# Last chunk of a graph layer: attention terms from unscaled rows, the 20-row tile ranked as columns, its X W made one pass later

## Chip, cores and metric

The kernel runs on one core of one Trainium2 chip. The metric is the device time of one launch in microseconds; the median of the runs shown is 1096.91 us.

## The reference

There are N = 2708 nodes with 128 features, a sparse non-negative matrix A (2708 x 2708), and four layers, each `x = layernorm(x + layer(x, A))`. The change lies where layer 0 ends and layer 1 begins.

```
layer 0:  y = d2 * x                      (d2 from the degrees and from 4 near neighbours S)
          out = d2 * ((S + A) @ y) @ W2 + b2
          x = layernorm(x + out)
layer 1:  XW = x @ W
          c = XW @ a[:128],  r = XW @ a[128:]            one number per node each
          den[i,j] = exp(leaky_relu(r[i] + c[j], 0.01))
          num = A @ den;   att = den / num
          H = A @ (att @ XW);   x = layernorm(x + H)
layers 2, 3: one product with A each
```

`den` has 2708 x 2708 entries, but r[i] + c[j] >= 0 or < 0 decides between two products of one-node terms. The kernel therefore sorts the nodes by c: it needs the rank of every c[j] among all of them, ties broken by the node's number.

## The kernel before

**Tiles, chunks, passes.** The nodes are cut into T = 22 tiles of 128 rows (the last, tile 21, has 20 rows) and C = 6 chunks of columns: four of 512, one of 384 (tiles 16 to 18), and the last of 276 (tiles 19, 20, 21). A transposed copy of A is streamed from memory panel by panel through a ring of four slots; six of its row tiles stay resident. A product of the whole of A with something 128 wide is a pass (`by_panels`, its matmul is L204). Pass 1 makes degrees and A x; then the neighbour stage finds four near nodes for every node (MAX8 and FIND_INDEX8 on VectorE, matmul L642 on TensorE); pass 2 makes (S + A) y; the third pass (`part_sum`, L1176) makes sums of A over runs of nodes in the order of c; then blocks of att are made and multiplied (block layer, L1423 and L1280), and three more passes follow.

**Order.** In pass 2 and after, the order on TensorE, VectorE and ScalarE is the order of the program (`manual_schedule`). In pass 2 the list `due` holds work by tick: one tick for each matmul of the pass, and `at(n, f, ...)` says at which tick `f` is issued. `end_pass2` files the work of a finished chunk; what is left when the matmuls end is issued by `due.flush()`, so that the whole tail of the last chunk comes then. GpSimd (POOL) and SyncE have their own queues, in order too. On each engine an instruction that waits holds back all behind it.

**What a chunk goes through.** `finish` adds the neighbour sums (`add_near`, L692) and copies the result to hT (L832). `norm0` multiplies by W2, adds to xs and normalizes: statistics on VectorE, the inverse root for the last chunk by POOL's pow (L253), then xs is scaled (L277). `turn` transposes xs (L737) and ScalarE copies it to xT (L739). `find_c` multiplies by a matrix whose columns all are W a (w_c, L744), so that c stands in every partition; ScalarE copies it to c_row (tile hT, L745), and VectorE picks the diagonals into cc (L749), one value per row. `times_w` makes X W and r (L757), `keep_xw` stores X W to memory through POOL (L763).

**Ranks.** `compare(t)` writes a mask: for each row of tile t, which columns up to its own tile have a c at least as large (L779; for tile 21 in the form that also sums, L774), and counts ties inside the tile (L781). `rank_rows` sums a mask along its rows on ScalarE (L792), `rank_columns` sums it along its columns on TensorE into rk (L797). After the flush, rk_f = after - rows_d - rk + rows_m is the rank (L918 to L923).

**From the ranks to the third pass.** `pick_c` finds the c at chosen ranks (L932 to L937), `to_all` spreads them over the partitions by a matmul (L943), `on_all` builds the row gb by 22 transposes of gb_col (L908) and six ScalarE copies (L915), and VectorE makes lc (L972 to L977), the weights of the third pass. `between(c, i0)` puts further work between its matmuls: at (0, 8) `find_blocks`, at (1, 4) the placing matmuls js (L1023), at (2, 4) `ranked`, which lets POOL clear xws and fetch X W rows in sorted order (L1047, L890). The matmul of lone_part (L1243) stands behind the first chunk's part sums.

**Buffers.** Masks have three buffers; small results go through `mis_tile`, three PSUM buffers in turn. `near` (128 x 22 x 8) is used by the neighbour stage only.

Of the kernel before, what the change touches and what calls it, by code (L numbers as in the profile page):

```python
# [8 lines left out]
F32 = mybir.dt.float32  # L9
U32 = mybir.dt.uint32  # L10
I32 = mybir.dt.int32
BF16 = mybir.dt.bfloat16
# [4 lines left out]
P = 128  # L17
# [13 lines left out]
class Due:  # L31
# [5 lines left out]
    def at(self, n, f, *args):  # L37
        self.work.append((n, len(self.work), f, args))
        self.work.sort(key=lambda w: w[:2])
# [13 lines left out]
def kernel(  # L53
# [213 lines left out]
    def normalize(ts, xs, power=False):  # L267

        t0, t1 = ts[0], ts[-1] + 1
        for t in ts:  # L270
            st = small.tile([P, 6], F32, tag="st", name="st")
            nc.vector.bn_stats(st[: pw[t]], xs[: pw[t], t, :])
            nc.vector.bn_aggr(mv[: pw[t], t, :], st[: pw[t]])
        rstd = small.tile([P, 4], F32, tag="rstd", name="rstd")
        inv_sqrt_of(rstd[:, : t1 - t0], mv[:, t0:t1, 1], LN_EPS, power)
        for t in ts:
            nc.vector.tensor_scalar(  # L277
                xs[: pw[t], t, :], xs[: pw[t], t, :], mv[: pw[t], t, 0:1], rstd[: pw[t], t - t0 : t - t0 + 1],
                op0=ALU.subtract, op1=ALU.mult,
            )  # L280
# [28 lines left out]
    def atile(shape, name, dt=F32):  # L309
        return att1.tile([P] + shape, dt, tag=name, name=name)  # L310
# [53 lines left out]
    with tc.tile_pool(name="knn", bufs=1) as knn:  # L364
# [185 lines left out]
            )  # L550
        w_c = atile([P], "w_c")
        nc.vector.tensor_copy(w_c, wae[:, D + 1 :].to_broadcast([P, P]))

        y2 = big.tile([P, T, D], F32, tag="y", name="y2")

# [147 lines left out]


    if LAST:
        nc.gpsimd.memset(xwe[:, FULL, :], 0.0)
        nc.gpsimd.memset(cc[:, FULL:], 0.0)


    c_row = hT  # L710
    rows_m = atile([T], "rows_m")
    rows_d = atile([T], "rows_d")
    nc.vector.memset(rows_d, 0.0)
    add_bias(b2_sb)
    rk = rk_pool.tile([P, T], F32, tag="rk", name="rk")

    def norm0(ts, power=False):
        po = mis_tile()
        for k, t in enumerate(ts):
            nc.tensor.matmul(  # L720
                po[: pw[t], k * D : (k + 1) * D], lhsT=hT[:, t * P : t * P + pw[t]], rhs=w2_sb, start=True, stop=True
            )
        for k, t in enumerate(ts):
            p = pw[t]
            nc.vector.scalar_tensor_tensor(
                xs[:p, t, :], po[:p, k * D : (k + 1) * D], d2inv[:p, t : t + 1], xs[:p, t, :],
                op0=ALU.mult, op1=ALU.add,
            )
        normalize(ts, xs, power)

    xTs, masks = {}, {}

    def turn(c):
        pt = mis_tile()
        for t in chunk_tiles[c]:
            o = t * P - starts[c]
            nc.tensor.transpose(pt[:, o : o + pw[t]], xs[: pw[t], t, :], ident[: pw[t], : pw[t]])  # L737
        xTs[c] = sum_pool.tile([P, CW], F32, tag="xT", name="xT", bufs=3)
        nc.scalar.copy(xTs[c][:, : cw[c]], pt[:, : cw[c]])  # L739

    def find_c(c):

# [17 lines left out]
    def keep_xw(c):  # L760
# [5 lines left out]
        if t1 <= ts[-1]:  # L766
            nc.gpsimd.dma_start(xw_rows[FULL * P :, :], xwe[:LAST, FULL, :D])

    def compare(t):
        p, o = pw[t], t * P  # L770
        s = cc[:p, t : t + 1]
        mask = masks[t] = sum_pool.tile([P, N], BF16, tag="mask", name="mask", bufs=3)
        if t in by_dve:
            nc.vector.tensor_scalar(  # L774
                mask[:p, : o + p], c_row[:p, : o + p], s, 0.0, op0=ALU.is_ge, op1=ALU.add,
                accum_out=rows_m[:p, t : t + 1],
            )
        else:
            nc.vector.tensor_scalar(mask[:p, : o + p], c_row[:p, : o + p], s, None, op0=ALU.is_ge)  # L779
        eq = small.tile([P, P], F32, tag="junk", name="eq")  # L780
        nc.vector.scalar_tensor_tensor(  # L781
            eq[:p, :p], c_row[:p, o : o + p], s, not_before[:p, :p], op0=ALU.is_equal, op1=ALU.mult,
            accum_out=rows_d[:p, t : t + 1],
        )

    by_dve = (T - 1,)

    def rank_rows(t):
        p, w = pw[t], t * P + pw[t]
        if t not in by_dve:  # L790
            junk = sum_pool.tile([P, N], BF16, tag="copy", name="junk")
            nc.scalar.activation(junk[:p, :w], masks[t][:p, :w], AF.Copy, accum_out=rows_m[:p, t : t + 1])  # L792

    def rank_columns(t):
        p = pw[t]
        for u in range(t):
            nc.tensor.matmul(  # L797
                rk[:, u : u + 1], lhsT=masks[t][:p, u * P : (u + 1) * P], rhs=ones_b[:p, :1],
                start=(t == 1 and u == 0), stop=(t == T - 1), skip_group_check=True,
            )  # L800


    def exp_table():
        tc.keep_in_program_order(nc.scalar.preload_act_table_set("natural_log_exp_and_others"))
# [1 line left out]
    gb_col = atile([T], "gb_col")  # L806

    def find_r():
        nc.vector.tensor_copy(rr, xwe[:, :, D])

    def exp_r():
        nc.scalar.activation(e_r, rr, AF.Exp)
# [12 lines left out]
    def end_pass2(c, acc):  # L825
        n = max(due.n + 1, near_at[chunk_tiles[c][-1]] + 3, ended[-1] + 16)
        ended.append(n)
        ts = chunk_tiles[c]

        def finish():  # L830
            add_near(c, acc)
            nc.scalar.copy(hT[:, cols[c]], acc[:, : cw[c]])  # L832

        at(n, finish)
        if c < C - 1:
            at(n + 2, norm0, ts)
            at(n + 9, turn, c)
            at(n + 11, find_c, c)
            for k, t in enumerate(ts):
                at(n + 13 + 2 * k, compare, t)  # L840
                at(n + 14 + 2 * k, times_w, c, t)
                if k == len(ts) - 1:
                    at(n + 14 + 2 * k, keep_xw, c)
                if c == C - 2 and k == len(ts) - 1:
                    behind_last.append(t)
                else:
                    at(n + 16 + 2 * k, rank_rows, t)
                if t:
                    at(n + 17 + 2 * k, rank_columns, t)
        else:  # L850
            for t in behind_last:
                at(n + 1, rank_rows, t)
            at(n + 1, exp_table)
            at(n + 2, norm0, ts, True)
            at(n + 3, turn, c)
            at(n + 4, find_c, c)
            for t in ts:
                at(n + 4, times_w, c, t)
            at(n + 4, keep_xw, c)
            for k, t in enumerate(ts):  # L860
                if k == len(ts) - 1:
                    at(n + 5 + k, find_r)
                at(n + 5 + k, compare, t)
                at(n + 5 + k, rank_rows, t)
                at(n + 6 + k, rank_columns, t)
            at(n + 6 + len(ts), exp_r)

    with tc.manual_schedule(engines={nc.tensor.engine, nc.vector.engine, nc.scalar.engine}):
        by_panels(
# [26 lines left out]
    with tc.tile_pool(name="rank", bufs=1) as rank:  # L896
        def rtile(shape, name, dt=F32):
            return rank.tile([P] + shape, dt, tag=name, name=name)

        lc = rtile([T, 32], "lc")  # L900
        order = ExitStack()
        order.enter_context(tc.manual_schedule(engines={nc.tensor.engine, nc.vector.engine, nc.scalar.engine}))

# [10 lines left out]
                ps, e = turned(col, n), min(row.shape[-1] - n * P, CW)  # L914
                nc.scalar.copy(row[:, n * P : n * P + e], ps[:, :e])  # L915

        rk_f = rtile([T], "rk_f")
        nc.vector.memset(rk_f, float(OOB))  # L918
        nc.vector.tensor_sub(after, after, rows_d)
        nc.vector.tensor_sub(after[:, : T - 1], after[:, : T - 1], rk[:, : T - 1])  # L920
        nc.vector.tensor_add(rk_f[:, : T - 1], after[:, : T - 1], rows_m[:, : T - 1])
        lp = pw[T - 1]
        nc.vector.tensor_add(rk_f[:lp, T - 1 :], after[:lp, T - 1 :], rows_m[:lp, T - 1 :])  # L923
        rk_psum.close()
        cnt_pool = psum.enter_context(tc.tile_pool(name="cnt", bufs=1, space=bass.MemoryType.PSUM))

# [20 lines left out]
        gb = wide.tile([P, T * D], F32, tag="wide", name="gb")[:, :N]  # L947
        on_all(gb, gb_col, 0, 8)
        c_head = to_all(head)
        on_all(gb, gb_col, 8, T)  # L950

        fold = rtile([2 * NCH], "fold")
        sel = rtile([2 * NB], "sel")
        neg_r = rtile([T], "neg_r")
        lone_part = rtile([1], "lone_part")
        lone_all = rtile([1], "lone_all")
        nc.vector.tensor_scalar_mul(neg_r, rr, -1.0)
        nc.vector.memset(lc[:, :, 2 * NCH :], 0.0)
        nc.vector.tensor_add(fold, ident[:, : 2 * NCH], ident[:, 32 : 32 + 2 * NCH])
        for g in (64, 96):  # L960
            nc.vector.tensor_add(fold, fold, ident[:, g : g + 2 * NCH])
        nc.vector.memset(sel, 0.0)
        nc.vector.tensor_copy(
            sel.rearrange("p (a v) -> p a v", v=2 * CH)[:, :, :2], fold.rearrange("p (a v) -> p a v", v=2)
        )

        c_cut = rtile([NCH], "c_cut")
        nc.vector.tensor_copy(c_cut, c_head[:, :NCH])
        nc.vector.memset(c_cut[:, 0:1], 3.0e38)
# [8 lines left out]
            lc_v[:, :, :, 1], cut, 0.5, f_r[:, :, None].to_broadcast(grid), op0=ALU.is_lt, op1=ALU.mult  # L978
        )
        spread(lc[:, FULL, :])  # L980

        c_part = pick_c(edge, "first")

        def whole(dst, src, n):

# [205 lines left out]

        def between(c, i0):

            if (c, i0) == (0, 8):
                c_edge = to_all(c_part)
                find_blocks(c_edge)
                work["js"] = js_pool.tile([P, CW], F32, tag="places", name="js")
# [421 lines left out]
```

## Time and profile before

| | us |
|---|---|
| median of 3 runs (1096.28 to 1101.85) | 1096.91 |
| the profiled execution, its own time | 1066.67 |
| its span, first to last instruction | 1064.9 |
| TensorE busy in the span | 993.3 |
| VectorE / ScalarE / POOL busy | 642.9 / 338.8 / 266.7 |
| pass 2, first to last matmul of L204 | 293.4 to 419.6 |
| third pass, first part sum to last sum copied | 443.15 to 503.4 |

The table is read against one execution: durations and places come from it, while the runs that give the median are timed without a profile. In the lines of the timelines the columns are start, duration, engine, source line, operation, what it writes and reads, count, and in brackets how long the engine had been idle and what released it. Matmuls are recorded in two halves for 32-bit data, so "x24" are twelve. PEld is TensorE's weight load.

### The profile page before, as it was taken

To read this page: it belongs to the slowest core of one execution; us is meant where nothing else is said; L and a number is where in the kernel's file an instruction comes from. 1 tells how busy PE (TensorE), PEld (TensorE's weight loads), DVE (VectorE), ACT (ScalarE), POOL (GpSimd) and SP (SyncE) were. 2 spreads that over 40 slices of the span, in tenths; PEclk is the share of its full clock that TensorE was granted. 3 is DMA by queue.
4 is the path that set the end of the run, shared out by engine and by line. 5 is a ranking of instruction groups with operands and counts; after the bars stand their busy time and mean duration, and the time that the engine had idled before them with its cause. 6 is when DMAs were issued, how large, how long until landed. Compare 5 with 4: busy or idle time off the path is not lost.

```text
span 1064.9 us, 11424 instructions
## 1 busy us (share of the span) xinstructions
PE 993.3 (93%) x3678; PEld 481.3 (45%) x3678; DVE 642.9 (60%) x1351; ACT 338.8 (32%) x614; POOL 266.7 (25%) x332
## 2 busy tenths in 40 slices
PE   0898999999999997699899999999999999999996
PEld 0345544444445566444333333334445544564444
DVE  6984438999965677853989999994111121222222
ACT  0000125555611246313767776662010100020000
POOL 4000000000457772117864444330121100000000
PEclk9999999999999998689999999999999999998998
DMA  9999340000168756388464555556665957574662
GB/s 340 374 339 267 104 156 1 0 1 1 34 215 268 224 172 225 136 318 266 133 181 130 139 143 161 143 162 223 203 211 152 315 166 227 145 262 149 222 175 65
DMA packets 109363, 190.30 MB, mean 179 GB/s; under 512 B 13650, under 2 KB 46690, under 8 KB 109294
## 3 DMA queue, kind: packets, MB, share of 16 engines
q1 hardware_dynamic: 91408, 151.79, 43.9%
q0 software_dynamic: 17712, 37.62, 12.8%
q8 instruction: 31, 0.51, 0.2%
q14 instruction: 38, 0.31, 0.1%
q10 hardware_dynamic: 174, 0.08, 0.0%
HBM read 214.37 MB, written 4.16 MB: 205 GB/s over the span
## 4 chain that ended last, share of the span: by engine, by line
PE 81%; DVE 5%; DMA 5%; POOL 3%; issue 3%; ACT 2%; SPq 1%; POOLq 0%; DVEq 0%; ACTq 0%
PE acc L204 36%; PE acc L642 9%; PE hacc L1280 9%; PE num L1423 8%; PE acc L428 7%; DMA res<-in_adjT 3%; PE acc L1176 2%; PE acc L632 2%; PE mis L285 1%; DMA part<-in_adjT 1%; DVE mask L779 1%; DMA ring<-in_adjT,slot_i 1%; DVE both L483 1%; POOL ring L125 1%; PE mis L1187 1%
## 5 line engine op out<-in xcount | busy, mean ns | idle before, releaser
L1301 POOL DMA_INDIRECT ring<-in_adjT,slot_i x88 | 98.2, 1116 | 100.8 <-PE num L1423 84.6
L1423 PE MATMUL num<-ring,lw 128*64 128x512 f32 (+1 forms) x528 | 113.6, 551 | 3.9 <-DVE err L1265 1.8
L1280 PE MATMUL hacc<-inv,xws 128*128 128x512 f32 (+1 forms) x264 | 111.7, 559 | 0.3 <-ACT inv L1258 0.3
L642 PE MATMUL acc<-zT,z 128*128 128x512 f32 (+4 forms) x264 | 108.6, 559 | 0.0
L1255 ACT ACTIVATE inv<-num,plain 128x1024 f32<-128x1024 f32 x88 | 80.5, 915 | 59.6 <-PE num L1423 57.5
L253 POOL TENSOR_TENSOR rstd<-rstd,minus_half 128x4 f32<-128x4 f32 (+1 forms) x19 | 18.2, 956 | 316.6 <-DVE rstd L252 316.6
L234 ACT COPY gb<-acc 128x512 f32<-128x512 f32 (+2 forms) x18 | 9.6, 534 | 252.7 <-PE acc L204 252.7
L643 ACT COPY key<-acc 128x512 f32<-128x512 f32 (+3 forms) x132 | 70.1, 534 | 59.9 <-issue 29.8
L204 PE MATMUL acc<-ring,y 128*128 128x512 f32 (+2 forms) x192 | 82.0, 557 | 0.5 <-POOL sim L579 0.5
L1265 DVE TENSOR_TENSOR err<-inv,num 128x1024 f32<-128x1024 f32 x88 | 74.2, 853 | 13.7 <-ACT inv L1258 12.9
L1280 PEld LDWEIGHTS hacc<-inv,xws 128*128 128x128 f32 x264 | 46.6, 190 | 77.3 <-issue 37.2
L204 PE MATMUL acc<-ring,xs 128*128 128x512 f32 (+2 forms) x192 | 78.2, 551 | 0.0
L672 POOL DMA_INDIRECT got<-y_rows,where x66 | 70.9, 1074 | 25.7 <-issue 9.1
L1272 DVE SCALAR_TENSOR_TENSOR inv<-gb,g_inv,inv 128x1024 f32<-128x1024 f32 x88 | 77.0, 912 | 0.1
L204 PE MATMUL acc<-ring,carry 128*128 128x512 f32 (+2 forms) x192 | 74.5, 542 | 0.0
L204 PE MATMUL acc<-ring,m_rows 128*128 128x512 f32 (+2 forms) x192 | 74.3, 542 | 0.0
L1269 DVE SCALAR_TENSOR_TENSOR inv<-err,inv 128x1024 f32<-128x1024 f32 x88 | 72.6, 863 | 0.1
L642 PEld LDWEIGHTS acc<-zT,z 128*128 128x128 f32 (+1 forms) x264 | 47.6, 188 | 54.9 <-issue 49.5
L1258 ACT ACTIVATE inv<-inv 128x1024 f32<-128x1024 f32 x88 | 67.6, 768 | 2.8
L644 DVE MAX8 near<-key 128x8 f32<-128x2708 f32 (+1 forms) x22 | 65.5, 2978 | 4.9 <-ACT key L643 4.9
L570 POOL TENSOR_TENSOR slot_e<-near,sim 128x44 f32<-128x44 f32 (+2 forms) x3 | 0.7, 241 | 270.0 <-DVE d2inv L598 265.8
L645 DVE FIND_INDEX8 where<-near,key 128x8 uint32<-128x2708 f32 (+1 forms) x22 | 65.4, 2972 | 0.0
(327 smaller groups left out, 1343.0 us busy)
## 6 DMA issues: line engine op xcount, KB each, us to landing
ring<-in_adjT SPq DMA_DIRECT2D x86, 1024.0 KB
ring<-in_adjT SPq DMA_DIRECT2D x19, 768.0 KB
part<-in_adjT SPq DMA_DIRECT2D x12, 1024.0 KB
ring<-in_adjT SPq DMA_DIRECT2D x19, 552.0 KB
res<-in_adjT SPq DMA_DIRECT2D x4, 1280.0 KB
more<-in_adjT SPq DMA_DIRECT2D x4, 1024.0 KB
part<-in_adjT SPq DMA_DIRECT2D x3, 768.0 KB
part<-in_adjT SPq DMA_DIRECT2D x3, 552.0 KB
```

Source lines behind the costliest of these rows:

```text
L204: nc.tensor.matmul(accs[c][: lhsT.shape[-1], :w], lhsT=lhsT, rhs=src, start=start, stop=stop)
L428: nc.tensor.matmul(accs[c][:, : cw[c]], lhsT=y[:, i, :], rhs=src[:, : cw[c]], start=first, stop=last)
L642: nc.tensor.matmul(pks[c][:p, : cw[c]], lhsT=z2[:, :p], rhs=zT[:, cs], start=False, stop=True)
L643: nc.scalar.copy(key[:p, cs], pks[c][:p, : cw[c]])
L672: nc.gpsimd.indirect_dma_start(out=got[:p, :], out_offset=None, in_=y2_rows[:, :], in_offset=bass.IndirectOffsetOnAxis(ap=where[:p, t, k : ...
L1255: nc.scalar.activation(inv, num[:, :w], AF.Ln, scale=plain[:, 0:1], bias=plain[:, 1:2])
L1265: nc.vector.tensor_mul(err, inv, num[:, :w])
L1269: nc.vector.scalar_tensor_tensor(inv, err, 2.0, inv, op0=ALU.subtract, op1=ALU.mult)
L1272: nc.vector.scalar_tensor_tensor(inv, gb[:, col : col + w], g_inv[:, q : q + 1], inv, op0=ALU.max, op1=ALU.mult)
L1280: nc.tensor.matmul(haccs[:, o:e], lhsT=xws[:, q, :], rhs=inv[:, o:e], start=(q == 0), stop=(q == NQ - 1))
L1301: nc.gpsimd.indirect_dma_start(out=rows[i][:KC, n, :], out_offset=None, in_=adj_half[:, :], in_offset=bass.IndirectOffsetOnAxis(ap=slot_i[ ...
L1423: nc.tensor.matmul(num[n * (BJ + 2) : (n + 1) * (BJ + 2), o:e], lhsT=lw[:, 2 * q + n, :], rhs=rows[i][:, n, c0 + o : c0 + e], start=True, ...
```

## The change

For the last chunk, `norm0(..., raw=True)` leaves the rows unscaled; they are transposed as they are, multiplied by two columns (w_rc = W a for r and for c), and `last_rc` makes c and r from the product, the mean times the column's sum (w_sum, one matmul in the neighbour stage) and the inverse deviation. `turn_c` transposes cc to get c_row. xs itself is scaled later, by `last_norm` behind the second `pick_c`, and its X W is made by `last_xw` in the third pass at (0, 4). Tile 21 has no mask row: `compare_few` compares all nodes with its 20 columns at once. Tile 20's mask is made in two halves, the second with its sum. The rank_columns calls come one or three ticks later and masks have four buffers. rk_f, neg_r, fold and sel live in the memory of `near` and are partly filled earlier; POOL clears the end of lc; two of the copies to gb come behind the weights lc.

```diff
         w_c = atile([P], "w_c")
         nc.vector.tensor_copy(w_c, wae[:, D + 1 :].to_broadcast([P, P]))
+        w_rc = wae[:, D:]
+        w_sum = atile([2], "w_sum")
+        ps = mis_tile()
+        nc.tensor.matmul(ps[:, :2], lhsT=ones_f, rhs=w_rc, start=True, stop=True)
+        nc.vector.tensor_copy(w_sum, ps[:, :2])
...
+    spare = near.rearrange("p t k -> p (t k)")
+    few_n, rk_f, neg_r = (spare[:, n * T : (n + 1) * T] for n in range(3))
+    fold, sel = spare[:, 3 * T : 3 * T + 2 * NCH], spare[:, 3 * T + 2 * NCH : 3 * T + 2 * NCH + 2 * NB]
+    nc.vector.memset(rk_f, float(OOB))
+    nc.vector.tensor_add(fold, ident[:, : 2 * NCH], ident[:, 32 : 32 + 2 * NCH])
...
+    def rc_of(c, p_of):
+        ts = chunk_tiles[c]
+        po = mis_tile()
+        for k, t in enumerate(ts):
+            p, o = p_of(t), t * P - starts[c]
+            nc.tensor.matmul(po[:p, 2 * k : 2 * k + 2], lhsT=xTs[c][:, o : o + p], rhs=w_rc, start=True, stop=True)
+        return po[:, : 2 * len(ts)].rearrange("p (k v) -> p v k", v=2)
...
+    def last_rc():
+        both = rc_of(C - 1, lambda t: P)
+        for v, dst in ((1, cc), (0, rr)):
+            nc.vector.scalar_tensor_tensor(
+                dst[:, l0:l1], mv[:, l0:l1, 0], w_sum[:, v : v + 1], both[:, v, :], op0=ALU.mult, op1=ALU.subtract
+            )
+            nc.vector.scalar_tensor_tensor(
+                dst[:, l0:l1], dst[:, l0:l1], -1.0, rstd_l, op0=ALU.mult, op1=ALU.mult
+            )
...
+    def turn_c(c):
+        pc = mis_tile()
+        for t in chunk_tiles[c]:
             o = t * P - starts[c]
+            nc.tensor.transpose(pc[:, o : o + P], cc[:, t : t + 1].to_broadcast([P, P]), ident)
+        nc.scalar.copy(c_row[:, cols[c]], pc[:, : cw[c]])
...
+    split = {T - 2: (T - 1) * P // 2}
...
-        mask = masks[t] = sum_pool.tile([P, N], BF16, tag="mask", name="mask", bufs=3)
+        mask = masks[t] = sum_pool.tile([P, N], BF16, tag="mask", name="mask", bufs=4)
+        m = split.get(t, o + p)
+        nc.vector.tensor_scalar(mask[:p, :m], c_row[:p, :m], s, None, op0=ALU.is_ge)
+        if m < o + p:
             nc.vector.tensor_scalar(
+                mask[:p, m : o + p], c_row[:p, m : o + p], s, 0.0, op0=ALU.is_ge, op1=ALU.add, accum_out=rows_h[:p],
+            )
+        own_ties(t)
...
+    def compare_few():
+        grid = [P, T, LAST]
...
+        nc.vector.tensor_tensor(
+            few_m, cc[:, :, None].to_broadcast(grid), c_row[:, None, FULL * P :].to_broadcast(grid), op=ALU.is_ge
+        )
+        for u in range(T):
+            nc.tensor.matmul(
+                rk[:LAST, T - 1 : T], lhsT=few_m[: pw[u], u, :], rhs=ones_b[: pw[u], :1], start=False,
+                stop=(u == T - 1), skip_group_check=True,
+            )
+        nc.vector.tensor_reduce(few_n, few_m, AX.X, ALU.add)
+        own_ties(T - 1)
...
                 if t:
-                    at(n + 17 + 2 * k, rank_columns, t)
+                    at(n + (20 if c < C - 2 else 18) + 2 * k, rank_columns, t)
...
-            at(n + 1, exp_table)
             at(n + 2, norm0, ts, True)
-            at(n + 3, turn, c)
-            at(n + 4, find_c, c)
-            for t in ts:
-                at(n + 4, times_w, c, t)
-            at(n + 4, keep_xw, c)
...
+            at(n + 2, turn, c, True)
+            at(n + 2, exp_table)
+            at(n + 2, find_r)
+            at(n + 3, last_stats)
+            at(n + 3, last_rc)
+            at(n + 3, turn_c, c)
+            at(n + 3, negate_r)
+            for k, t in enumerate(ts[:-1]):
+                at(n + 4 + k, compare, t)
+                at(n + 4 + k, rank_rows, t)
+                at(n + 5 + k, rank_columns, t)
+            at(n + 3 + len(ts), compare_few)
+            at(n + 4 + len(ts), exp_r)
...
+        nc.gpsimd.memset(lc[:, :, 2 * NCH :], 0.0)
...
-        on_all(gb, gb_col, 8, T)
+        on_all(gb, gb_col, 8, 16)
...
         spread(lc[:, FULL, :])
+        on_all(gb, gb_col, 16, T)
         c_part = pick_c(edge, "first")
+        last_norm()
+
+        def last_xw():
+            for t in last_ts:
+                p = pw[t]
+                pt = mis_tile()
+                nc.tensor.transpose(pt[:, :p], xs[:p, t, :], ident[:p, :p])
+                xT = small.tile([P, P], F32, tag="z", name="xT")
+                nc.scalar.copy(xT[:, :p], pt[:, :p])
+                po = mis_tile()
+                nc.tensor.matmul(po[:p, :D], lhsT=xT[:, :p], rhs=wa_sb, start=True, stop=True)
+                row = small.tile([P, P], F32, tag="junk", name="row")
+                nc.scalar.copy(row[:p], po[:p, :D])
+                nc.gpsimd.dma_start(xw_rows[t * P : t * P + p, :], row[:p])
...
         def between(c, i0):
+            if (c, i0) == (0, 4):
+                last_xw()
```

The weighing of the ranks itself (`find_ranks`) has the same terms as before, with the counts of `compare_few` for tile 21, in seven small operations.

## The prediction

> **What bounds the kernel now.** I read the windows first, then the chain of waits, then each engine's timeline from 405 to 505 us, where the edits lie. The windows (columns: PE, PEld, DVE, ACT, POOL busy us, granted TensorE clock, DMA share, GB/s):
>
> ```profile
> 420.00:425.00 5.00, 2.05 (x28) 1.44 (x26) 2.10 (x10) 4.82 (x7) 1.01 (x2) 0.79 0.78 241
> 430.00:435.00 5.00, 1.58 (x41) 1.19 (x39) 5.00 (x8) 3.80 (x4) 2.97 (x2) 0.50 0.10 28
> 435.00:440.00 5.00, 3.13 (x32) 2.74 (x33) 4.02 (x17) 2.93 (x7) 0.00 (x0) 0.50 0.00 0
> 445.00:450.00 5.00, 5.00 (x42) 1.23 (x34) 4.66 (x17) 0.00 (x0) 0.00 (x0) 1.00 0.91 310
> 450.00:455.00 5.00, 2.75 (x15) 0.85 (x12) 4.86 (x11) 0.65 (x2) 0.00 (x0) 0.87 1.05 388
> ```
>
> TensorE is the bound nearly everywhere (993.3 of 1064.9 us), except between the second and third pass: from 421 to 443 it waits for one chain through VectorE, ScalarE and itself, at half clock, and DMA is idle too. It stops once more, at 450. The timelines show that chain:
>
> ```profile
> 422.44 0.85 DVE L725 SCALAR_TENSOR_TENSOR xs<-mis,d2inv,xs 128x128 f32<-128x128 f32 x3 [2.50 <-PE mis L720]
> 425.70 0.85 DVE L277 TENSOR_SCALAR xs<-xs,mv,rstd 128x128 f32<-128x128 f32 x3 [1.02 <-POOL rstd L253]
> 429.27 0.29 DVE L749 SCALAR_TENSOR_TENSOR own<-mis,ident 128x128 f32<-128x128 f32 x1 [2.73 <-ACT hT L745]
> 429.80 1.54 DVE L779 TENSOR_SCALAR mask<-hT,cc 128x2560 bf16<-128x2560 f32 x1
> 433.42 3.02 DVE L774 TENSOR_SCALAR_CACHE_REDUCE mask<-hT,cc 20x2708 bf16<-20x2708 f32 x1
> 438.05 0.41 DVE L932 TENSOR_TENSOR head<-rk_f,edge 128x242 f32<-128x242 f32 x1
> ```
>
> ```profile
> 439.91 3.31 PE L908 MATMUL mis<-ident,gb_col 128*128 128x128 f32 x14
> 443.15 2.89 PE L1176 MATMUL acc<-ring,lc 128*32 128x512 f32 x24
> 452.24 0.35 PE L1243 MATMUL mis<-lone_part,ones_f 128*128 128x1 f32 x2 [2.16 <-DVE lone_part L1223]
> 457.31 5.05 PE L1023 MATMUL js<-val_q,hot_in 128*128 128x44 f32 x36
> ```
>
> The reader is to see: the mask of the 20-row last tile costs as much as two full ones (3.02 us); the first part sum at 443.15 comes right behind 14 transposes of PE, not behind DVE's lc (done at 441.92); and PE idles 2.16 us for lone_part, the end of a DVE queue that runs without a gap from 437.35.
>
> **What the Trainium skill says.** "TensorE: Matmul & The Clock Gate", Part 1, says that the array runs at half rate after a window of about 3.4 us with little matmul work and at full rate after a busy one, the windows running free. The trace agrees: the clock falls at 423.0, rises at 443.5, falls at 453.7 (behind the lone_part wait), rises at 457.1, falls at 460.5 (behind the 44-wide js matmuls) and rises at 467.3, on a 3.41 us grid. "VectorE: DVE Perf Modes", section on the TRN2 errata, says that an instruction pays a fixed cost besides its elements. The trace agrees: 128x3 takes 0.17 us, 128x22 0.18, 128x242 0.41, 128x968 1.16.
>
> **The change part by part** (times on the clock of the profile before).
>
> 1. *Before the last chunk.* fold, sel and a memset move into VectorE's neighbour stage (DVE busy 99.26 of 100 us at 180 to 280), four of them ahead of the last y2 rows: 0.08 + 3 x 0.18 = about 0.5 us later. The gathers on POOL (first at 307.39, behind the y2 store) follow, and add_near of the first chunk (326.44 to 327.33, its last operand ready at 326.94) has some 0.2 us to spare: +0.3 us (0 to 0.5). w_sum is one tiny matmul and a copy: PE's own wait of 0.70 us at 164.11 covers it, else 0.3. In pass 2 rank_columns go later on PE. The 2.16 us stall at 408.71 mostly comes back as a wait of the w_c matmul (L744) for ACT's xT, which ends at 412.40; that matmul began at 413.05, so up to 0.6 us, less what a cold window then takes: -0.3 (0 to -0.6). The fourth mask buffer removes a DVE wait of 0.44 us at 365 that was off the path. Sum 0 (-0.6 to +0.5): chunk 5's hT copy stays at 420.92.
>
> 2. *c from raw rows.* Before: xs ends 423.29, statistics and POOL's pow end 425.67, then scaling, transposes (0.95), xT, w_c (1.29), hT, three own diagonals, mask at 429.80. After: the raw transposes (423.35 to 424.3), xT (0.47) and three 2-wide matmuls (about 0.8 at half clock, from the 11-wide L943) end at 425.6, beside statistics and pow, now 0.1 later at 425.8. Then one 128x3 product 0.2, three transposes 1.0, hT copy 0.4 plus 0.05: mask at 427.55. The rest (rr, neg_r) fits beside the transposes. The table load of 1.28 ends at 425.8, ahead of the hT copy. Gain 2.25 (1.7 to 2.7).
>
> 3. *The comparisons.* Before, mask 429.80 to head 438.05: 8.25. After: tile 19, 1.73; tile 20 halved, 0.85 plain + 1.55 with sum (half of the 3.02 row) + 0.3 ties; few_m 440 wide 0.6, its reduction 0.6, ties 0.2; seven small operations of find_ranks 1.2. Sum 7.03, gain 1.2 (0.6 to 1.7). ACT's sums (2.43, then 1.3, then three exps) end at 433.2 and PE's 22 narrow matmuls at 433.1, both ahead of their use at about 434. Head at 434.6.
>
> 4. *Head to first part sum.* fold, sel, neg_r and the lc memset leave DVE (1.17 us), but PE binds here: c_head and 14 transposes still stand ahead of the part sums, 438.05 to 443.15, and again 5.10. Gain 0; DVE's lc is ready at 438.05, 1.6 us before. The lc memset on POOL (0.25, by its xwe memset of 0.20) waits for an old mask buffer and is done by 434. First part sum at 439.7, 3.45 us earlier.
>
> 5. *X W in the third pass.* New on PE behind eight part sums: transpose, ACT copy, matmul, ACT copy, for three tiles. Each PE matmul waits for its ACT copy, and the next tile's transpose is queued behind it: 0.33 (a transpose of L737, 0.95 / 3) + 0.27 (ACT's 129-wide L758) + 0.22 (step from one L757 matmul to the next) + two hand-overs of 0.04 (PE to ACT 0.02 and ACT to PE 0.06 at 427) = 0.9, 2.7 in all (2.5 to 3.5 cold). last_norm sits on DVE behind c_part_first (441.45) and adds 0.85 to its queue; PE arrives at 441.7 warm or 443.2 cold, so it waits 0 to 0.6. The next part sum starts near 445.0. Before it was 445.1: here the 3.45 us are spent. Removed from the old path: three times_w (1.61 PE, hidden). POOL's three stores (0.8 to 1.8 each) come about 446 to 450 in a POOL idle of 41 us, far ahead of the fetches at 477. SP's panel loads follow PE's part sums, go on during X W, and are slack (DMA share 0.48 at 460).
>
> 6. *The lone_part wait.* DVE from c_part_first to lone_part took 452.10 - 445.39 = 6.7; now 441.45 + 0.85 + 6.7 = 449.0. PE gets there at 445.0 + 5.0 = 450.0 and finds it done: the stall of 2.16 us goes. Next late is nothing; PE is bound by itself.
>
> 7. *Clock.* The cold window behind the old wait (453.7 to 457.1, about 1.7 us lost) goes; a sparse stretch of the same length (X W) makes another. Taken as 0, with 1.7 either way for each of two windows. POOL's chain at 474.62 (memset, 14 fetches, ring loads), which bounds the start of the block layer, hangs on js, so it moves with PE.
>
> **Sum:** 0 - 2.25 - 1.2 + 0 + about 3.3 (X W, its wait and the half-cold start) - 2.0 (rest of the stall) = **-2.2 us**: span 1062.7, and the profiled run's own 1066.67 becomes 1064.5. The median of the runs (1096.91) stands 30.24 above that run; taken as unchanged, 1094.7.
>
> **Rivals.** (a) *The clock stays up:* first part sums warm, no cold window behind X W. Then lone_part's matmul is reached at 439.7 + 2.0 + 2.9 + 4.9 = 449.5 (-2.7), the window at 453.7 stays warm (-1.7), and js costs one cold window less (-1.7): 1090.8. For it: part sums are dense. Against: X W leaves PE about half idle, and 2.45 busy of 3.41 us was too little at 419.6 to 423. (b) *X W costs more than the ranking saves:* three cold turns 3.5, 0.6 wait for last_norm, 1.5 for a cold start, 3.4 for two cold windows of part sums, 9.0 together, against 3.45 + 2.16 + 1.7: +1.7, 1098.6, slower. It decides once X W and its windows take over 5.6 us (7.3 if the old cold window goes). For it: the serial turns are certain. (c) *It doesn't do what it says:* the rank chain stays, if PE, cold, delays rc_of or the c transposes past POOL's pow, or c_row waits behind the table load; steps 2 and 3 give 1 us, X W takes it: 1096.9.
>
> **How the numbers follow.** Chances: likeliest case 0.55, (a) 0.2, (b) 0.15, (c) 0.1. The range takes both ends of the clock (3.4) and of steps 1 to 3 (about 2) around 1094.7: 1089.0 to 1100.0. 0.5%, about what a measurement of this kernel can tell from no change, is 5.5 us: only most of (a) and its tail pass it downwards, little of (b) upwards: faster 0.22, within 0.70, slower 0.08.
>
> **What would show it.** Right: first part sum about 3.4 us earlier against the hT copy; the lone_part matmul without a wait; six X W instructions strung over about 3 us with ACT as releaser; a second mask instruction of about 1.5 us in place of 3.02. Wrong: PE waiting for DVE, or a first part sum less than 2 us earlier (steps 2 and 3), an end of the third pass that moved by over 5 us (step 7), or POOL fetches waiting for the new stores (step 5).

## The result, and the profile after

| comparison | before, median | after, median | ratio after / before, 95% |
|---|---|---|---|
| the first, 19 runs of each | 1099.17 us | 1096.47 us | 0.9991 (0.9977 to 1.0006) |
| beside the experiments, 48 and 14 runs | 1062.91 us | 1065.96 us | 1.0013 (0.9988 to 1.0039) |

The change makes no difference that can be told from none: -1.0 us (-2.5 to +0.7) in the first comparison, +1.4 us (-1.3 to +4.1) in the second. The forecast was -2.2. These differences follow the ratios, which are not the quotients of the two medians; the medians alone differ by -2.7 and +3.0 us, so not even the sign is settled.

For both kernels the medians of the first comparison lie above those of the second, by 36 us (before) and 31 us (after), and the profile of before (span 1064.9) is of the lower level while the first one of the changed kernel (span 1093.3) is of the higher. So both kernels have a second profile, taken side by side: *before_again*, span 1059.8, and *after_again*, span 1067.3. In these two the second MAX8 of the neighbour stage starts at 174.34 and 174.29 us and pass 2 at 294.01 and 293.76, so their clocks can be laid over each other to within 0.3 us. All "after" lines below are of after_again.

These windows answer to those of before (columns as there); the tail now lies from 428 to 446 us:

```profile
430.00:435.00 5.00, 2.92 (x30) 2.10 (x30) 3.06 (x16) 2.76 (x5) 0.90 (x1) 0.75 1.03 389
435.00:440.00 5.00, 1.99 (x58) 1.74 (x59) 4.97 (x10) 3.89 (x6) 0.00 (x0) 0.50 0.11 41
440.00:445.00 5.00, 4.66 (x30) 4.18 (x27) 3.84 (x19) 2.05 (x6) 0.28 (x1) 0.50 0.00 0
445.00:450.00 5.00, 4.02 (x26) 1.78 (x25) 4.79 (x12) 2.19 (x7) 0.00 (x0) 0.88 0.31 73
450.00:455.00 5.00, 4.39 (x37) 1.74 (x37) 4.79 (x13) 0.89 (x5) 1.73 (x3) 1.00 1.05 396
```

The tail is of the same kind as before, TensorE waiting at half clock, but shorter. ("Cold" below means at half clock, "warm" at full clock.) VectorE's timeline of after_again through it:

```profile
429.52 0.85 DVE L742 SCALAR_TENSOR_TENSOR xs<-mis,d2inv,xs 128x128 f32<-128x128 f32 x3 [2.50 <-PE mis L737]
434.49 1.55 DVE L841 TENSOR_SCALAR mask<-hT,cc 128x2560 bf16<-128x2560 f32 x1 [0.94 <-ACT hT L804]
436.23 0.92 DVE L841 TENSOR_SCALAR mask<-hT,cc 128x1344 bf16<-128x1344 f32 x1
437.06 1.61 DVE L843 TENSOR_SCALAR_CACHE_REDUCE mask<-hT,cc 128x1344 bf16<-128x1344 f32 x1
438.86 0.62 DVE L875 TENSOR_TENSOR few_m<-cc,hT 128x440 bf16<-128x440 f32 x1
441.18 0.41 DVE L1024 TENSOR_TENSOR head<-near,edge 128x242 f32<-128x242 f32 x1
```

And TensorE's, from the last transposes of gb_col to the matmul of lone_part (transposes are recorded whole here, so x14 are fourteen):

```profile
443.04 3.23 PE L1006 MATMUL mis<-ident,gb_col 128*128 128x128 f32 x14
446.20 1.92 PE L1270 MATMUL acc<-ring,lc 128*32 128x512 f32 x16
448.68 0.30 PE L1069 MATMUL mis<-ident,xs 128*128 128x128 f32 x1 [0.56 <-DVE xs L793]
450.35 0.49 PE L1073 MATMUL mis<-w_att,xT 128*128 128x128 f32 x2 [0.41 <-ACT xT L1071]
451.50 1.02 PE L1270 MATMUL acc<-ring,lc 128*32 128x512 f32 x5
456.49 0.38 PE L1339 MATMUL mis<-lone_part,ones_f 128*128 128x1 f32 x2
```

From xs to the mask of tile 19 takes 5.0 us in place of 7.4; the 3.02 us mask of 20 rows has become 1.61 for half of tile 20; X W waits 0.56 us for last_norm and goes on from copy to copy; and lone_part's matmul shows no wait, where it had 2.16. The tail does what was forecast. The two profiles beside each other show where its gain goes:

| us | before_again | after_again | difference |
|---|---|---|---|
| last MAX8 of the neighbour stage, start | 294.78 | 297.01 | +2.2 |
| first gather of pass 2, start | 308.19 | 311.58 | +3.4 |
| pass 2, first to last matmul of L204 | 126.70 | 133.24 | +6.5 |
| last hT copy to first part sum | 22.25 | 18.21 | -4.0 |
| first part sum to the matmul of lone_part | 9.10 | 10.29 | +1.2 |
| from there to the last copy of tot | 46.28 | 47.82 | +1.5 |

In these profiles pass 2 gives back more than the tail gains. The sizes are those of two single executions: the one of after_again (1068.98 us) is 3.0 above the median of its runs, that of before_again (1061.49) 1.2 below its own.

The loss begins in the neighbour stage. In before_again VectorE goes on there without a gap. Its timeline, behind a MAX8 that ends at 285.74:

```profile
285.78 0.09 DVE L645 MATCH_VALUE_LOAD where<-near,key 128x8 f32 x1
```

VectorE's timeline of after_again at the same place:

```profile
282.54 2.96 DVE L649 MAX8 near<-key 128x8 f32<-128x2708 f32 x1
287.92 0.16 DVE L723 TENSOR_TENSOR near<-ident 128x22 f32<-128x22 f32 x1 [2.41 <-issue]
290.95 2.96 DVE L649 MAX8 near<-key 128x8 f32<-128x2708 f32 x1
```

And GpSimd's at the same time:

```profile
283.84 3.82 POOL L607 TENSOR_TENSOR y<-xs,d2inv 128x2176 f32<-128x2176 f32 x1
287.62 0.24 POOL L583 TENSOR_TENSOR slot_e<-slot_e,near 128x33 f32<-128x33 f32 x1
287.96 1.58 POOL L615 DMA_DIRECT2D y_rows<-y  x1
```

L722 and L723 write rk_f and fold, which the change puts into the memory of near. L583 on GpSimd still reads the eq values of near's first eleven tiles there, and it is queued behind a multiplication of 3.82 us. It ends at 287.86; VectorE goes on at 287.92, after 2.41 us without work, with two MAX8 and their index searches queued behind. The profile names no releaser ("issue"); the two times do, and they do so again in two other kernels that write there (289.13 and 289.19 in before_near_wait, 287.26 and 287.33 in add_near_later). From there the delay goes through the last y2 rows and their store to the gathers, and TensorE meets it at add_near of the first chunk. In TensorE's timeline of before_again the products of the chunk's four tiles (eight halves) run through:

```profile
327.11 1.05 PE L692 MATMUL acc<-ident,near_sum 128*128 128x128 f32 x8
```

In after_again's the third waits a little and the fourth long:

```profile
326.86 0.61 PE L697 MATMUL acc<-ident,near_sum 128*128 128x128 f32 x4
327.71 0.49 PE L697 MATMUL acc<-ident,near_sum 128*128 128x128 f32 x2 [0.24 <-DVE near_sum L690]
331.02 0.80 PE L697 MATMUL acc<-ident,near_sum 128*128 128x128 f32 x2 [2.83 <-DVE near_sum L690]
331.61 3.62 PE L204 MATMUL acc<-res,y 128*128 128x512 f32 x4
```

The windows of after_again around it, 3.4 us each:

```profile
326.40:329.80 3.40, 1.55 (x8) 0.90 (x6) 1.29 (x4) 0.00 (x0) 2.62 (x3) 1.00 1.03 364
329.80:333.20 3.40, 2.18 (x4) 1.26 (x5) 0.95 (x4) 1.33 (x2) 2.66 (x3) 0.55 0.77 274
333.20:336.60 3.40, 3.40 (x11) 2.25 (x10) 1.01 (x3) 0.54 (x1) 2.49 (x4) 0.50 0.16 42
336.60:340.00 3.40, 3.40 (x10) 1.73 (x10) 2.85 (x13) 0.00 (x0) 2.79 (x3) 0.95 0.23 58
```

The wait of 2.83 us empties most of one window and part of the next, and the clock (the seventh number, after the five busy times) stays near one half for two of them; in before_again it is 1.00 in all four. "TensorE: Matmul & The Clock Gate", Part 1, of the Trainium skill says that the array goes to half rate after an idle window. Here a window need not be idle: 1.55 and 2.18 us of work in 3.40 were already too little. One such wait costs this profile 6.5 us in pass 2, over twice its own length. These are readings of two profiles. The experiments test them.

### The profile page after: what moved, and what is told of

It reads as the page before. It is cut to its first block, busy times and chain, and to the rows that moved or that the text cites. A ratio compares the mean times of both kernels' runs of the same rounds, so it can differ in the third digit from the quotient of the medians.

```text
span 1093.3 us, 11460 instructions
## 1 busy us (share of the span) xinstructions
PE 1001.2 (92%) x3691; PEld 483.3 (44%) x3691; DVE 641.2 (59%) x1354; ACT 338.3 (31%) x617; POOL 262.2 (24%) x334
## 4 chain that ended last, share of the span: by engine, by line
PE 79%; DVE 7%; DMA 6%; issue 4%; ACT 2%; POOL 1%; another core or an unknown queue 1%; SPq 1%; POOLq 0%; DVEq 0%; ACTq 0%
PE acc L204 32%; PE num L1519 9%; PE hacc L1376 9%; PE acc L647 8%; PE acc L428 7%; DMA res<-in_adjT 3%; PE acc L1270 3%; PE acc L637 2%; DMA got<-y_rows,where 1%; PE mis L285 1%; DVE where L650 1%; DMA part<-in_adjT 1%; DVE near L649 1%; DVE both L483 1%
## 5 line engine op out<-in xcount | busy, mean ns | idle before, releaser
L204 PE MATMUL acc<-ring,y 128*128 128x512 f32 (+2 forms) x192 | 81.3, 554 | 0.5 <-POOL sim L584 0.5
L204 PE MATMUL acc<-ring,xs 128*128 128x512 f32 (+2 forms) x192 | 77.2, 545 | 0.0
L204 PE MATMUL acc<-ring,carry 128*128 128x512 f32 (+2 forms) x192 | 74.5, 542 | 0.0
L204 PE MATMUL acc<-ring,m_rows 128*128 128x512 f32 (+2 forms) x192 | 74.3, 542 | 0.0
```

The costliest lines, as they stand in the source:

```text
L204: nc.tensor.matmul(accs[c][: lhsT.shape[-1], :w], lhsT=lhsT, rhs=src, start=start, stop=stop)
```

## The experiments

Times are medians of one comparison with its own runs of before (1061.7 to 1062.9 us); a ratio is to before, with its 95% interval. 0.5% is 5.3 us. The comparisons ran on three chips, so two edited kernels of different comparisons are set against each other by their ratios to before. Stage times are of the profiled execution.

**Both kernels again**

before_again is the kernel before, unedited.

> The kernel before, unedited, for a second profile. Its first profiled execution had a span of 1064.9 us, 30 us under each of its timed runs, and the difference to the changed kernel's profile (28 us) opens between 311 and 443 us. Theory A: that is the execution and not the change; the new profile has a span near 1095, pass 2 ends near 443 us instead of 419 us, with waits of 5 to 10 us of TensorE and VectorE between 326 and 370 us as in the changed kernel. Theory B: the change itself costs some 24 us in pass 2 and gains as much elsewhere; the new profile has pass 2 ending near 419 us.

> The changed kernel, unedited, beside the kernel before on one chip. If theory A holds, its stages differ from the fresh profile of before by: last MAX8 and first gather +2.5 to +4 us, hT copy of the last chunk to first part sum -3.5 to -3.7, part sums to the js matmuls +0.5 to -2. Time: within 3 us of before.

Measured: before_again 1062.71 us, ratio 1.0007 (0.9991 to 1.0023); after_again 1065.96 us, 1.0013 (0.9988 to 1.0039). Pass 2 ends at 420.7 in before_again, so theory A is wrong as it stood: the wait at add_near is the change's own. Theory B's 24 us is wrong too: 6.5 is what pass 2 loses between these two; the changed kernel's first profile has another 16.7 in pass 2 that its second does not have. Of after_again's expected differences, MAX8 and gather (+2.5 and +3.6 against the start of pass 2) and part sums to js (13.62 against 14.19 us, -0.6) came; the tail gained 4.0 in place of 3.5 to 3.7.

**The wait alone, put into the kernel before**

```diff
+    spare = near.rearrange("p t k -> p (t k)")[:, : 22]
+    nc.vector.memset(spare, float(OOB))
+    nc.vector.tensor_add(spare, ident[:, :22], ident[:, 32:54])
     nc.vector.memset(rows_d, 0.0)
```

> The kernel before with two operations added ahead of its rows_d memset on VectorE: a memset of 128x22 and a sum of two stretches of ident, both written to the memory of near. They do what the change's first operations do, and nothing else of it is made. Theory 1: VectorE stands about 2.4 us behind GpSimd's reads of near, and the kernel is 2 to 4 us slower than before. Theory 2: the stall shows, the time stays within 1 us of before.

Measured: 1069.41 us, ratio 1.0052 (1.0037 to 1.0068), 5.5 us slower (3.9 to 7.2). VectorE's timeline of before_near_wait:

```profile
289.19 0.07 DVE L645 MATCH_VALUE_LOAD where<-near,key 128x8 f32 x1 [2.42 <-issue]
289.20 0.08 DVE L714 MEMSET near<- 128x22 f32 x1
```

And TensorE's, at add_near:

```profile
332.29 0.53 PE L692 MATMUL acc<-ident,near_sum 128*128 128x128 f32 x2 [2.86 <-DVE near_sum L685]
```

Two operations of 0.08 and 0.17 us cost 5.5. Theory 1 names the mechanism, but its 2 to 4 us are too low: only the lower end of the interval reaches them. Pass 2 takes 131.18 us, 4.5 more than in before_again: 2.86 of wait, and one cold window, from 332.6 to 336.0 (3.4 x 0.50 = 1.7 us). Here the wait (329.4 to 332.3) lies inside one window, 329.2 to 332.6. In after_again it (328.2 to 331.0) lies across the edge of two, 330.1, and both windows up to 336.9 run cold. TensorE still waits in the first 0.9 us of them, so they cost about (6.8 - 0.9) x 0.5 = 3.0 us (an estimate), 1.3 of the 2.1 us by which its pass 2 is longer still.

The delay grows on its way: MAX8 is 2.4 us late against the start of pass 2, the first gather 3.6, because GpSimd waits 5.86 us for the store of the last y2 rows to land in place of 4.68.

**The wait alone, taken out of the change**

A tile of their own for these operations, at the same place in the program (own_tiles), does not fit: a later pool needs 8 kb per partition, and 7.47 are left. So no run keeps their place and changes only their memory. Instead they become a function that is issued in pass 2:

```diff
+    def prepare():
-    nc.vector.memset(rk_f, float(OOB))
+        nc.vector.memset(rk_f, float(OOB))
...
+    at(40, prepare)
```

> The changed kernel with one edit: the memset of rk_f and the sums and copies into fold and sel are issued in pass 2 (at tick 40) and no longer in the neighbour stage; all stays in the memory of near. Theory 1 (the wait of VectorE behind GpSimd's reads of near is what costs): in the changed kernel TensorE waits 2.83 us for near_sum at 331 us and then loses about 1.7 us in a window at half clock; both go, pass 2 is shortened from 133.2 us to about 128.7, and the time is 4 to 5 us below the changed kernel's, 3 to 4 below before. Theory 2 (the loss in pass 2 comes from the later rank_columns, or the gathers are late for another reason): pass 2 stays above 131 us and the time within 1.5 us of the changed kernel's.

Measured: 1058.4 us, ratio 0.9957 (0.9942 to 0.9972), 4.6 us faster than before (3.0 to 6.2) and 5.9 below the changed kernel (by the two ratios; about 3 to 9, an estimate from their intervals). Last MAX8 at 294.56, first gather at 307.88, and TensorE's timeline of prepare_later:

```profile
326.88 1.05 PE L697 MATMUL acc<-ident,near_sum 128*128 128x128 f32 x8
```

All eight halves run without a wait; pass 2 takes 126.98 us, even less than expected. Theory 1 holds. The same operations (0.9 us of VectorE) in the same memory, issued in pass 2, leave pass 2 at 126.98 us, against 126.70 in before_again.

**The late gathers kept, add_near later**

The wait on VectorE stays; TensorE comes to add_near of chunk 0 five ticks later:

```diff
-        n = max(due.n + 1, near_at[chunk_tiles[c][-1]] + 3, ended[-1] + 16)
+        n = max(due.n + 1, near_at[chunk_tiles[c][-1]] + (8 if c == 0 else 3), ended[-1] + 16)
```

> The changed kernel with one number altered: the neighbour sums of chunk 0 (add_near) are issued five ticks later, at near_at + 8 in place of near_at + 3; the wait of VectorE in the neighbour stage stays, and the gathers stay late. Theory 1 (the late gathers cost time only because TensorE stands 2.83 us at this add_near and then runs a window at half clock, 1.7 us): last MAX8 and first gather stay where they are in the changed kernel (297.0 and 311.6 us), the wait at add_near goes, pass 2 takes 128 to 130 us in place of 133.2, and the time is 3 to 5 us below the changed kernel's. Theory 2 (the late gathers hold pass 2 up elsewhere too, through the got buffers and VectorE): the wait only moves to a later chunk, pass 2 stays above 131.5 us and the time within 2 us of the changed kernel's.

Measured: 1056.79 us, ratio 0.9929 (0.9900 to 0.9958). GpSimd's timeline of add_near_later shows that the first gather is still late:

```profile
310.84 1.14 POOL L677 DMA_INDIRECT got<-y_rows,where  x1 [5.68 <-DMA y_rows<-y]
```

TensorE's shows that the wait is small now:

```profile
330.55 0.83 PE L697 MATMUL acc<-ident,near_sum 128*128 128x128 f32 x6
332.20 0.49 PE L697 MATMUL acc<-ident,near_sum 128*128 128x128 f32 x2 [0.82 <-DVE near_sum L690]
332.53 1.88 PE L204 MATMUL acc<-ring,y 128*128 128x512 f32 x4
```

Pass 2 takes 127.96 us, and TensorE's clock is 1.00 from 323 to 343. Theory 1 holds: the late gathers cost time at this one instruction, and a number in the list of ticks takes most of it away without touching VectorE. The time lies further below the changed kernel's than the 3 to 5 us expected (8.9 by the two ratios, from 7 runs); why is not shown.

**Both cures**

> The changed kernel with both edits, the preparations in pass 2 (prepare_later) and add_near of chunk 0 five ticks later (add_near_later). Theory 1 (they are two cures of one loss, the wait at this add_near and its cold window): together they give no more than one of them, pass 2 takes 127 to 128 us and the ratio to before lies at 0.993 to 0.996 like either alone. Theory 2 (each takes a loss of its own away): the gains add, pass 2 takes under 126 us and the ratio is under 0.991.

Measured: 1057.49 us, ratio 0.9941 (0.9917 to 0.9964), pass 2 126.84 us. The gains do not add: theory 1, one loss with two cures. The intervals of the three overlap, so none of them is shown to be the best; by the ratios each beats both kernels.

**The ticks of rank_columns**

```diff
-                    at(n + (20 if c < C - 2 else 18) + 2 * k, rank_columns, t)
+                    at(n + 17 + 2 * k, rank_columns, t)
```

> As prepare_later, and rank_columns back at the tick of before (n + 17 + 2k for every chunk). Theory 1 (the delay only moved a wait: 2.17 us for the mask in rank_columns became 2.64 us for xT at the w_c matmul of chunk 4, and cost part of a clock window): the wait stands at rank_columns again, pass 2 takes 126.5 to 127.5 us, and the time is 1 to 2 us below prepare_later. Theory 2 (the later ticks gain a little, as was forecast, -0.3): pass 2 is 0 to 0.6 us longer than in prepare_later.

Measured: 1058.3 us, ratio 0.9958 (0.9940 to 0.9975), the same as prepare_later. In its profile TensorE waits 2.17 us at rank_columns and 0.92 at the w_c matmul; in prepare_later 0.24 and 2.65. So the later ticks move a wait from the mask to xT. Pass 2 is 1.0 us shorter with the old ticks (125.97), the direction of theory 1, but the first part sum comes at 439.46 and 439.60, and the time shows nothing: theory 1's 1 to 2 us did not come, and a few tenths either way can't be told from zero.

**X W: two gaps, or none**

At (0, 4) three transposes and one copy, at (0, 8) three matmuls and the copies out:

```diff
             if (c, i0) == (0, 4):
-                last_xw()
+                work["xT_l"] = turn_last()
             if (c, i0) == (0, 8):
+                last_xw(work["xT_l"])
```

> As prepare_later_old_ticks, and the X W of the last chunk is made in two gaps: at (0, 4) three transposes into one PSUM tile and one copy to xT_l, at (0, 8) three matmuls into one PSUM tile, three copies out, three stores. Theory 1 (X W costs mostly hand-overs between TensorE and ScalarE): TensorE no longer waits there, first part sum to the lone_part matmul falls from 10.3 us to about 9 us or less, and the time is 1 us lower, up to 3 if a clock window stays warm. Theory 2 (that stretch is bound by VectorE's queue up to lone_part and find_blocks): a wait for lone_part of 1 to 2 us comes back, and the time doesn't move.

The other kernel leaves X W out and stores rows of xs in its place:

```diff
             for t in last_ts:
-                p = pw[t]
...
-                nc.gpsimd.dma_start(xw_rows[t * P : t * P + p, :], row[:p])
+                nc.gpsimd.dma_start(xw_rows[t * P : t * P + pw[t], :], xs[: pw[t], t, :])
```

> As prepare_later_old_ticks, but X W of the last chunk is left out: rows of xs are stored in its place, so six TensorE instructions and six ScalarE copies in the third pass are gone and the three stores stay. It prices X W. Theory 1 (X W costs about 2.7 us of chain less what it covers of the wait for lone_part): first part sum to the lone_part matmul falls by 1 to 2.7 us, with a wait for lone_part of up to 2.2 us back; the time is 1 to 2 us below prepare_later_old_ticks. Theory 2 (X W also makes cold clock windows): the js matmuls start over 3 us earlier against the first part sum and the time is 3 to 5 us lower.

Measured: in two gaps 1056.92 us, ratio 0.9964 (0.9950 to 0.9978); without X W 1058.19 us, 0.9960 (0.9946 to 0.9975); with X W as the change has it (prepare_later_old_ticks) 0.9958. First part sum to lone_part's matmul takes 9.69, 9.83 and 10.30 us. TensorE's timeline without X W shows why so little comes back:

```profile
449.19 0.35 PE L1333 MATMUL mis<-lone_part,ones_f 128*128 128x1 f32 x2 [2.98 <-DVE lone_part L1313]
```

Without X W TensorE waits for lone_part again, 2.98 us. X W fills a wait for VectorE's queue: it adds 0.5 us to the stretch and nothing to the time that the runs show. Behind the unfilled wait the clock falls for one window (0.52 from 449.6 to 453.0), so that without X W js even comes later, 14.95 us behind the first part sum in place of 13.62; with X W that window stays warm and a later one is cold (0.54 from 456.4 to 459.8 in prepare_later_old_ticks). That is theory 2 of xw_in_two_gaps, though its wait there was 0.25 us and not 1 to 2. Of xw_no_compute's theories, the first saw the wait, but its 1 to 2 us were not there; the second is wrong: in these two profiles X W moves a cold window and adds none.

**The old ranking of the last tiles**

```diff
-            for k, t in enumerate(ts[:-1]):
+            for k, t in enumerate(ts):
                 at(n + 4 + k, compare, t)
...
-            at(n + 3 + len(ts), compare_few)
```

with `compare`, `rank_rows`, `rank_columns` and the sum of the ranks as they were before.

> As prepare_later, with the ranking of the last tiles as it was before: tile 20 one plain mask, tile 21 a mask with its sum (20 rows x 2708), no compare_few, the ranks found by the five old operations. What is left of the change is c from unscaled rows, X W in the third pass and the moved preparations. It parts the two gains of the tail. In prepare_later mask of tile 19 to head takes 6.68 us, before 8.25; the hT copy of the last chunk to that mask 7.1 and 9.1. Theory 1 (both gain as measured in the traces): mask to head returns to 8.2 us, first part sum comes 1.5 us later against the end of pass 2 than in prepare_later (20.3 us in place of 18.8), and the time lies 1.5 us above it. Theory 2 (the first part sum is bound by the 14 transposes of gb_col behind ScalarE's exponentials, not by head): head moves by 1.5 us, the first part sum by under 0.5, and the time doesn't move.

Measured: 1060.15 us, ratio 0.9976 (0.9957 to 0.9994). VectorE's timeline has the old instruction back:

```profile
431.20 3.02 DVE L843 TENSOR_SCALAR_CACHE_REDUCE mask<-hT,cc 20x2708 bf16<-20x2708 f32 x1
435.59 0.41 DVE L1025 TENSOR_TENSOR head<-near,edge 128x242 f32<-128x242 f32 x1
```

Mask of tile 19 to head takes 7.93 us (6.68 in prepare_later), hT copy to first part sum 19.72 (17.94), and the ratio is 0.0019 higher, 2.0 us, though the intervals overlap, so the runs alone do not show it. Theory 1 holds in the profile: from head to the first part sum 5.02 us pass in both kernels, so what the comparisons gain reaches the part sums in full. The gain of c from raw rows has no run of its own; it is read from the profiles, where hT copy to mask takes 8.9 us in the kernels that lack it and 6.2 to 6.8 in those that have it.

## Why the prediction was wrong

The forecast of no measurable difference, and the range, held. The size didn't (-2.2 against -1.0 and +1.4). That the total came near is luck: it is the sum of a gain of some 4 to 5 us and a loss of some 6 that the prediction did not have. Every sign of being right that it named came, for all of them look at the tail.

- **Step 1 failed, before the last chunk, "+0.3 (0 to 0.5)".** This is the term that was mis-sized. It was made of durations (four operations, 0.5 us) and of 0.2 us to spare at add_near. The operations write into near, and the prediction did not ask who still reads it: GpSimd, behind 3.81 us of y2 that the profile of before shows as well. Measured: VectorE 2.4 us late, the first gather 3.4, pass 2 +6.5 us in the profiles; 5.5 us (3.9 to 7.2) in the runs when put in alone, 5.9 when taken out alone. Even with the wait known, a gather 3.4 us late less the 0.2 to spare would have given about 3; the rest is the cold clock behind the stall. Step 7, which gave clock windows 1.7 either way, counted only those of the tail.
- **Step 1, rank_columns, "-0.3 (0 to -0.6)".** The wait does come back at the w_c matmul as was said, but as 2.64 us in place of 2.17; the runs show no gain and no loss.
- **Step 2, c from raw rows, 2.25.** hT copy to mask went from 8.89 to 6.50 us: 2.4. Right.
- **Step 3, the comparisons, 1.2 (0.6 to 1.7).** Mask to head 8.25 to 6.69: 1.56. The old ranking gives 1.25 back in its own profile. Right, at the upper side.
- **Step 4, head to first part sum, 0.** 5.11 to 5.02. Right: TensorE's transposes bind. The three steps together were 3.45 and measured 4.0.
- **Step 5, X W, 2.7 and a wait of 0 to 0.6.** From the first transpose at 448.68 to the next part sums pass 2.6 to 2.8 us (the first of them are recorded at 451.28, before the last X W matmul), and the wait for last_norm is 0.56. Right.
- **Step 6, the lone_part wait.** Gone. Steps 5 and 6 were 3.3 - 2.0 = +1.3 and measured +1.2.
- **Step 7, the clock, 0 (1.7 either way, twice).** From lone_part's matmul to the last copy of tot, 46.28 us became 47.82, and prepare_later takes 44.51; the first profile of before takes 49.6. These four have one, two, no and three cold windows there, and the profiles of the edited kernels fall on the same steps (44.5 to 44.7 us with none, 46.1 to 46.3 with one): each costs 1.5 to 1.8 us. So the +1.5 of the table is one window more. The spread is inside what was allowed.

With step 1 taken out, the change is worth 4.6 us (3.0 to 6.2) where steps 2 to 6 promised 2.2. Its profile reaches lone_part's matmul 3.4 us before before_again does, 1.2 more than forecast; behind it that profile has one cold window less.

Of the rivals, (b), X W as a loss, is refuted by leaving X W out, which gives no time back. (a) came in part in after_again: no cold window follows X W (clock 1.00 from 450 to 460), but the clock then falls to 0.50 from 465 to 470. (c) is refuted by steps 2 and 3. None of them put the loss into the neighbour stage.

Two things stay open. Why the first comparison takes over 30 us more was not tried. In the changed kernel's first profile the excess over after_again lies in pass 2 (149.99 us against 133.24) and in the third pass up to the last tot (67.63 against 58.11); no profile of before with so long a span exists. The wait at add_near is there too, 4.76 us in place of 2.83, but what it costs there is not known.

## What to carry to other kernels

An operation that is moved into old memory takes on every reader of that memory, on every engine: before pricing it by its duration, look up the last reader of those bytes and what is queued ahead of that reader. Where an engine has no idle time, as VectorE here at 99% busy, it hands a delay on in full; follow it to the first place where the bounding engine would meet it, and price it there with the clock that comes after. And a preparation that is needed late belongs where its engine is idle anyway, not at the earliest place.

## What the runs showed that I had not expected

- A delay grows twice on its way: 2.4 us on VectorE became 3.6 at the first gather (5.86 us of waiting for the y2 store in place of 4.68), shrank to 2.86 at TensorE, and became 4.5 through the clock. Why the store takes longer is not shown: the DMA engines were busy 94% of the ten microseconds from 300, and 90% before, but in add_near_later 86% with a wait of 5.68.
- A wait of 2.98 us was filled with 2.8 us of new work on the waiting engine at a price of 0.5 us: six small TensorE instructions and six ScalarE copies, chained one behind the other, show no cost in the time.
- A stall of 2.8 to 3.0 us in a dense stretch made one cold window where it lay inside one (before_near_wait, xw_no_compute) and two where it lay across an edge (after_again), at some 1.3 us more. What a stall costs depended on where the windows fell.
